# Edge-list operations on VectorE in four of eight slots instead of seven

## The chip, the cores and the metric

The kernel runs on one core of a Trainium2 chip. The core has five engines with instruction queues of their own: TensorE (PE in the profile; PEld are its weight loads), VectorE (DVE), ScalarE (ACT), GpSimd (POOL) and SyncE (SP), which issues most DMA transfers. Each queue is worked off in the order in which the kernel's program wrote it; a queue waits for another one by semaphores. The metric is the device time of one execution in microseconds. Three runs of the kernel before took 14773.6, 14776.33 and 14777.28 us; the median is 14776.33 us.

## The reference, cut to what matters

Three layers follow each other. Layer 0 is two Mamba passes (over 96 time steps, then over 32 variables) on 4 x 32 x 96 rows of 256 channels. Layer 1 has an additive attention and a graph-routed mixture of experts. Here M = 12288 rows, four batches of 3072, and 1048576 edges.

```python
# attention: every query against every key of its batch
h = tanh(q[:, :, None, :] + k[:, None, :, :] + bh)      # 3072 x 3072 x 32 per batch
a = softmax(einsum('biju,u->bij', h, Wa) + ba)
v = einsum('bij,bjd->bid', a, inputs)
# graph attention over edges (src, dst), with a loop edge for every row
e   = leaky_relu(a_src[src] + a_dst[dst], 0.2)
ee  = exp(e - segment_max(e, dst)[dst])
agg = segment_sum(h[src] * ee / segment_sum(ee, dst)[dst], dst) + b_gat
# gates: top 2 of 4 experts from layernorm(agg); then the experts
out = sum_e gate_e * (gelu(x @ W1[e] + b1[e]) @ W2[e] + b2[e])
```

The edge indices are drawn from 0 to 65535, while there are only 12288 rows. In JAX an index past the end is clamped when gathered, and dropped when used as a target of a segment sum. So most edges have the last row as source, and most have no target at all. The kernel makes lists of the edges that matter: one of edges with a real source and target, and one that only counts, per target, the edges whose source was clamped.

## The kernel before, in words

**Order.** The program writes the order of PE, ACT, DVE and POOL by hand. `Attention.units` is the clock of it. It walks over i, one **slot** each: in a slot ACT makes one tanh of a 128 x 3072 tile `th` (L1031; four queries at a time), and PE turns the tile of two slots earlier (LAG = 2) into scores (`scores`, L1004). Eight slots make a **unit** of 32 queries. The slots of a unit are numbered here by k = (i - 2) mod 8, the place of the score product that is made in the slot. `th` has three buffers, the score bank `pe` one, and the bank `pv`, which transposes and values share, one.

A unit ends so (`unit_tail`). In slot 7, after the scores, DVE takes the maximum (`nb`, L1087, "the reduce"), and ACT the exponential (`pr`, L1094). In slot 0 of the next unit PE transposes four blocks of `pr`, in slot 1 the other two, and in slot 2 it multiplies by the values (`pv`, L1110). Each of these is followed one slot later by a DVE copy out of the bank: `pT` in slots 1 and 2 (L1103), `pvs` in slot 3 (L1112). The copies are kept in `self.later` and written into DVE's queue early in the slot. Every fourth unit ends a tile of 128 queries; then `tile_tail` adds small steps in slots 3 to 7 (factors `g` and `f`, with one small exponential on ACT, L1165).

**What runs beside it.** `units` yields twice in a slot: after the tanh and after the scores. At each yield the generator `steps` in `whole` goes on. While layer 0 lasts, that is layer 0. When layer 0 has ended, the loop at L2254 takes turns:

- At the first yield of a slot it writes **list operations** of `Edges.sort` into DVE's queue. So they stand ahead of the copies of that slot, and ahead of the scores and the reduce. `sort` yields after every operation or few, with its cost in microseconds as the program's author put it down. `us_v` is the budget: it gets EDGE_US = 2.3 in each slot except slot 7 (`att.reduces`), each yielded cost is taken off, and a debt is carried on to the next slot while credit is not.
- At the second yield it writes count products of the one-hot tiles (`ed.todo`), index gathers on POOL (`columns`), and parts of the experts (`Experts.early`) by a second budget `us_t` of SLOT_US = 1.2 per slot. The experts' parts are PE products into `ph` and `po`, with a DVE bias step after them: `h` (L1933, 128 x 512) and `ko` (L1945, 128 x 512). `po` has one bank at this time, so the next product into it waits for `ko`.

**The list operations.** `sort` reads the edges in four quarters. For each quarter, 16 pieces of 256 columns are loaded by DMA into a tile `e` with two buffers and narrowed to 16 bits (L1368). Then `compact` moves the kept entries of 2048 columns to the front, eleven levels of bit, predicated copy (L1314) and up to three products or sums (L1318, L1321, L1323). A fifth compaction of 2048 columns, two of 384 and eight of 392 follow, and some index arithmetic. Up to here there are 894 yields, with costs of 480.1 us in all. Then `self.listed` is set and 232 one-hot pairs follow (L1473), each with 1.195 us of cost, limited by how fast the count products take them (`len(ed.todo) < 2`).

**Afterwards.** `units` runs out after 3072 tanhs. Then `tail` finishes the graph and the remaining experts.

Of the kernel before, what the change touches and what calls it, by code (L numbers as in the profile page):

```python
# [45 lines left out]
LAG = 2  # L46
# [14 lines left out]
G1, K1 = 8, 4  # L61
GP, GG = 12, 4
EDGE_US = 2.3
GATHER_US, HALF_US, GROUP_US, LAND_US = 1.6, 2.7, 2.0, 10.0
QUARTERS = 2, 0, 3, 1
KO_BUFS = 2
# [773 lines left out]
class Attention:  # L840
# [4 lines left out]
    def __init__(self, ctx, tc, ident, a, x1, x2, xn2T, tab_s, tab_a, keys, l0):  # L845
        self.nc = nc = tc.nc
        self.ident, self.x1, self.x2, self.xn2T = ident, x1, x2, xn2T
        self.tab_s, self.tab_e, self.tab_a = *tab_s, tab_a
        pool = lambda name, bufs, **k: ctx.enter_context(
            tc.tile_pool(name=name, bufs=bufs, side="right", **k))  # L850
        const = self.const = pool("atc", 1)
        self.rows, self.th, self.wk = pool("atr", 2), pool("atb", TH_BUFS), pool("atw", 1)
        self.ps_e = pool("ate", PE_BUFS, space=PSUM)
        self.ps_v = pool("atv", PV_BUFS, space=PSUM)

        def load(name, shape, ap):
            t = const.tile(shape, F32, tag=name, name=name)
            nc.sync.dma_start(t, ap)
            return t

        self.l0, self.kq, self.krep, self.qsel = l0, keys, keys.krep, keys.qsel
        self.wa = load("wa_blk", [P, P // (4 * R_ATT), QU], a["wa_blk"])
        self.ba = load("ba_rep", [P, 1], a["ba_rep"])
        self.wg = load("wg", [P, KC, HF], a["W_gat"].rearrange("(k p) f -> p k f", p=P))
        self.asr = load("as_rep", [P, HF], a["as_rep"])
        self.adr = load("ad_rep", [P, HF], a["ad_rep"])
        self.eps = const.tile([P, 1], F32, tag="eps1", name="eps1")
        nc.vector.memset(self.eps, 1e-5)

        self.sel = const.tile([P, QU], F32, tag="sel", name="sel")  # L870
        nc.vector.tensor_tensor(self.sel, ident[:, :QU], ident[:, QU:2 * QU], ALU.add)
        for q in range(2, P // QU):
            nc.vector.tensor_tensor(self.sel, self.sel, ident[:, q * QU:(q + 1) * QU], ALU.add)
        self.state = [{} for _ in range(B)]

        self.extra, self.entry, self.col, self.asked, self.normed = 0.0, 0, 0, 0, 0
        self.now, self.reduces = None, False
        self.mark = const.tile([P, 1], F32, tag="mark", name="mark")

        self.later = []  # L880
# [111 lines left out]
    def units(self, side):  # L992


        nc = self.nc
        todo, behind = [], []
        NK = QU // R_ATT
        PER = TOK // R_ATT

        def scores(pe, k, th):  # L1000
            for j in range(2):
                for q in range(NQT):
                    c0 = q * KQ + j * KQ // 2
                    nc.tensor.matmul(pe[q * QU:(q + 1) * QU, j, :KQ // 2], self.wa[:, k, :],  # L1004
                                     th[:, c0:c0 + KQ // 2], start=(k == 0), stop=(k == NK - 1))

        def beside():
            while side:
                try:
                    return next(side[0])  # L1010
                except StopIteration:
                    side.pop(0)

        i = 0
        while i < B * PER + LAG or todo or self.later:
            b, col = self.entry, self.col = divmod(i, PER)
            if self.waits(b, col):

                yield
                late, self.later = self.later, []
                for f in late:
                    f()
                yield
                beside()
                continue
            if b < B:
                s = self.state[b]
                th = self.th.tile([P, TOK], F32, tag="th", name="th")  # L1030
                nc.scalar.activation(th, s["krep"], AF.Tanh, bias=s["qsel"][:, col:col + 1])  # L1031
                behind.append(th)
                self.now = th
            self.reduces = behind and (i - LAG) % NK == NK - 1
            yield
            late, self.later = self.later, []
            for f in late:
                f()
            busy = tail = None
            if behind and i >= LAG:  # L1040
                n, k = divmod(i - LAG, NK)
                if k == 0:
                    pe = self.ps_e.tile([P, 2, JB], F32, tag="pe", name="pe")
                scores(pe, k, behind.pop(0))
                if k == NK - 1:
                    tail = self.unit_tail(*divmod(n, TOK // QU), pe)
                    busy = True

            self.extra = 0.0 if tail or not todo else getattr(todo[0], "us", 0.0)
            yield  # L1050
            if tail:

                for f in todo:
                    f()
                todo = tail()
            elif todo and hasattr(todo[0], "us"):
                if not todo[0].full:
                    beside()
                todo.pop(0)()
                busy = True  # L1060
            elif todo:
                todo.pop(0)()

            if b < B and col == LAG + 3:
                self.load_values(b)
            if b < B and LAG + 4 <= col < LAG + 10:
                self.normalize_values(b, col - LAG - 4)
            if b and col == LAG + 10:
                side.append(self.after(b - 1, *AFTER[-1]))
            side += [self.after(b, t0, t1) for t0, t1 in AFTER[:-1]  # L1070
                     if b < B and col == t1 * P // R_ATT + LAG + 10]
            if busy is None:
                beside()
            i += 1
        side.append(self.after(B - 1, *AFTER[-1]))
# [156 lines left out]
class Edges:  # L1232
# [97 lines left out]
    def sort(self):  # L1330
# [4 lines left out]
        with ExitStack() as ctx:  # L1335
# [157 lines left out]
            while self.todo:  # L1493
                yield EDGE_US
            v.tensor_copy(self.cnt, pc)
# [339 lines left out]
class Experts:  # L1835
# [62 lines left out]
    def output(self, h, q0, w2):  # L1898
        po = self.bank(self.ps_o, [P, 2, C], "po")
        for q in range(2):  # L1900
# [3 lines left out]
            yield po  # L1904

    def early(self, units, a, place):


# [299 lines left out]
def whole(tc, a, dram, out):  # L2208
# [12 lines left out]
    with ExitStack() as ctx:  # L2221
        actx, lctx, ectx = ExitStack(), ExitStack(), ExitStack()
        with tc.manual_schedule(engines={E.PE, E.Activation, E.DVE, E.Pool}):
# [5 lines left out]
            att, side = None, []  # L2229
            late = {}  # L2230

            def steps():
                nonlocal att

                for done in l0.run():
                    if done is not None:
                        b, i = done
                        if att is None and i == max(PARTS):
                            att = Attention(actx, tc, ident, a, x1, x2, xn2T, (tab_s, tab_e), tab_a,
                                            keys, l0)  # L2240
# [8 lines left out]
                ed = late["ed"] = Edges(ctx, ectx, tc, a, tab_e, tab_a)  # L2249
# [2 lines left out]

                us_v = us_t = 0.0
                while True:  # L2254
                    us_v = min(us_v, 0.0) + (0.0 if att.reduces else EDGE_US)
                    while lists and us_v > 0 and len(ed.todo) < 2 and "krep" in att.state[B - 1]:
                        us = next(lists, None)
                        if us is None:
                            lists, late["listed"] = None, True
                        else:  # L2260
                            us_v -= us
                    yield
                    if columns is None and ed.listed and att.normed >= B - 1:
                        columns, turn = ed.columns(), 1
                    if columns:
                        att.pace()
                        turn = 3 - turn
                        for f, k, c in columns[:turn]:
                            f(k, c)
                        del columns[:turn]  # L2270
                    us_t = min(us_t, SLOT_US) + SLOT_US - att.extra
                    if ed.todo and us_t > 0:
                        ed.todo.pop(0)()
                        us_t -= G1 * PRODUCT_US
                    if units is None and att.entry == B - 1 == att.normed:

                        units = late["units"] = ex.early(
                            [(i, e) for i in range(NBLK_X - NBLK_X // B) for e in range(NEXP)
                             if (i, e) not in ex.done], a, att.krep[B % 2])
                    while units and us_t > 0:  # L2280
                        us_t -= next(units, 1.0) or 0.0
                    yield

            flow = steps()
            while not side:
                next(flow)
# [96 lines left out]
```

## Time and profile before

| what | value |
|---|---|
| median of three runs | 14776.33 us |
| the profiled execution's own time | 14803.64 us |
| span, first to last instruction | 14801.9 us |
| mean granted TensorE clock | 0.897 |
| list operations in DVE's queue (first load to first one-hot) | 11303 to 12168 us |
| one-hots | 12168 to 13355 us |
| last reduce of the attention | 13857 us |

The profiled execution took 27.3 us longer than the median of the runs. "Busy" is the time in which an engine worked; "idle before" is the time an engine stood still ahead of a group of instructions, with the name of what ended most of it. A wait is put down to the semaphore that came last. DVE, ACT and POOL start their instructions in the queue's order, so an instruction that waits holds up all behind it.

### The profile page before, as it was taken

The page shows a single profiled execution, that of the slowest core. Times are in us where ns is not written, and L with a number is a line of the kernel's source. Part 1 is how long each engine was busy: PE and PEld are TensorE (multiplying, and loading weights), DVE is VectorE, ACT ScalarE, POOL GpSimd, SP SyncE. Part 2 cuts the span into 40 slices and gives each one's busy share as a digit, 9 for nine tenths or more (in the row PEclk, how much of TensorE's full clock was granted, in tenths as well). Part 3 has the DMA queues.
Part 4 walks back from the last instruction along what each step waited for, and adds up shares of the span by engine and source line. Part 5 has one row for each costly group of instructions (what it writes and reads, how often), then busy time and mean ns, then how long its engine had stood idle before and what let it go on. Part 6 is the DMA issues. An engine that isn't in the chain of part 4 may idle for free.

```text
span 14801.9 us, 224787 instructions
## 1 busy us (share of the span) xinstructions
PE 11378.9 (77%) x86704; PEld 5164.8 (35%) x86704; DVE 10505.3 (71%) x15265; ACT 12306.2 (83%) x9676; POOL 9078.2 (61%) x7108
## 2 busy tenths in 40 slices
PE   5777767777777777778887777788876778988888
PEld 2333332222222333333333233333332334443466
DVE  7888887777777777777778777667786783331376
ACT  3445559999999899999998899999998889999522
POOL 5777767777777667777676677657762005550272
PEclk8888988888888888899998888999988999999999
DMA  6777765445455444455554444445542000010233
GB/s 208 228 228 229 230 198 148 148 149 151 149 152 154 147 146 149 152 153 153 151 153 147 151 148 149 131 127 150 155 148 89 27 19 13 9 22 18 60 105 117
DMA packets 1206752, 1984.20 MB, mean 134 GB/s; under 512 B 419364, under 2 KB 655396, under 8 KB 1200548
## 3 DMA queue, kind: packets, MB, share of 16 engines
q1 hardware_dynamic: 1174948, 1963.77, 43.4%
q0 software_dynamic: 30720, 5.96, 0.8%
q8 instruction: 682, 11.17, 0.3%
q14 instruction: 402, 3.29, 0.1%
HBM read 1859.14 MB, written 110.18 MB: 133 GB/s over the span
## 4 chain that ended last, share of the span: by engine, by line


## 5 line engine op out<-in xcount | busy, mean ns | idle before, releaser
L1031 ACT ACTIVATE th<-krep,qsel 128x3072 f32<-128x3072 f32 x3072 | 8676.3, 2849 | 373.6 <-PE pe L1004 346.7
L1004 PE MATMUL pe<-th,wa_blk 128*32 128x384 f32 x49152 | 5026.5, 536 | 1633.0 <-ACT pr L1094 1528.5
L514 POOL TENSOR_TENSOR h<-h,bC 128x768 f32<-128x768 f32 x2048 | 3766.0, 1840 | 2718.9 <-DVE h L507 2267.0
L507 DVE TENSOR_TENSOR_SCAN h<-dA,dB 128x384 f32<-128x384 f32 x3008 | 2707.2, 941 | 862.6 <-ACT dA L469 629.1
L1004 PEld LDWEIGHTS pe<-th,wa_blk 128*32 128x32 f32 x49152 | 1471.5, 116 | 4140.5 <-issue 1932.0
L482 DVE TENSOR_TENSOR dB<-bB,dtu 128x768 f32<-128x768 f32 x1912 | 1812.4, 948 | 207.1 <-ACT dtu L557 134.5
L521 POOL TENSOR_TENSOR h<-h 128x768 f32<-128x768 f32 x752 | 1414.4, 1881 | 53.6
L533 PE MATMUL py<-h,ident 128*128 128x384 f32 x2176 | 946.9, 567 | 485.9 <-POOL h L514 485.1
L469 ACT ACTIVATE dA<-dt,t_A 128x380 f32<-128x380 f32 x2048 | 1118.4, 569 | 216.1 <-DVE h L507 131.2
L469 ACT ACTIVATE dA<-dt,d_A 128x372 f32<-128x372 f32 x2048 | 1103.7, 562 | 133.0 <-DVE h L502 61.4
L1110 PE MATMUL pv<-xn,pT 128*32 128x257 f32 x18432 | 1104.1, 387 | 127.3 <-DVE pT L1103 126.9
L502 DVE TENSOR_TENSOR_SCAN h<-dA,dB 128x768 f32<-128x768 f32 x544 | 947.7, 1751 | 144.8 <-ACT dA L469 93.8
L1169 POOL TENSOR_SCALAR sf<-sel,f 128x32 f32<-128x32 f32 x384 | 151.1, 417 | 1296.9 <-ACT f L1165 1296.4
L1103 DVE COPY pT<-ptw 128x512 f32<-128x512 f32 (+1 forms) x768 | 420.5, 548 | 683.6 <-PE ptw L1101 672.8
L1110 PEld LDWEIGHTS pv<-xn,pT 128*32 128x32 f32 x18432 | 582.2, 112 | 708.7 <-DVE pT L1103 255.1
L522 POOL TENSOR_TENSOR h<-h 128x384 f32<-128x384 f32 x752 | 783.8, 1042 | 59.0
L523 POOL TENSOR_TENSOR y<-y,h 128x384 f32<-128x384 f32 x752 | 777.2, 1033 | 59.0
L533 PEld LDWEIGHTS py<-h,ident 128*128 128x128 f32 x2176 | 424.6, 212 | 952.2 <-POOL h L514 726.6
L1087 DVE TENSOR_REDUCE nb<-pe 128x1 f32<-128x768 f32 x384 | 363.2, 946 | 446.5 <-PE pe L1004 428.6
L1253 POOL DMA_INDIRECT gd<-tab_a,di x480 | 491.3, 1024 | 165.3 <-issue 162.3
L1101 PE MATMUL ptw<-ident,pr 128*128 128x128 f32 x2304 | 473.6, 323 | 100.4 <-DVE pT L1103 45.7
L1112 DVE COPY pvs<-pv 128x257 f32<-128x257 f32 x384 | 159.8, 416 | 516.4 <-PE pv L1110 462.5
(326 smaller groups left out, 15255.2 us busy)
## 6 DMA issues: line engine op xcount, KB each, us to landing
bB<-bc SPq DMA_DIRECT2D x2048, 384.0 KB
bC<-bc SPq DMA_DIRECT2D x2048, 384.0 KB
x<-x SPq DMA_DIRECT2D x321, 128.0 KB
all<-kept SPq DMA_DIRECT2D x40, 1024.0 KB
kept<-ko SPq DMA_DIRECT2D x43, 512.0 KB
xt<-xn2T SPq DMA_DIRECT2D x41, 512.0 KB
qsel<-xn2T SPq DMA_DIRECT2D x75, 256.0 KB
kept<-eo SPq DMA_DIRECT2D x150, 128.0 KB
```

Source lines behind the costliest of these rows:

```text
L469: nc.scalar.activation(inner(dA[:, s * T:(s + 1) * T] if alone else self.dA[s][:, :T]), inner(blk["dt"][:, e, :]), AF.Exp, scale=blk["w"][ ...
L482: nc.vector.tensor_tensor(dB, blk["bB"].pop(j), z["dtu"].unsqueeze(1).to_broadcast([P, SB, T]), ALU.mult)
L502: nc.vector.tensor_tensor_scan(flat(h), dA[:, :SB * T], flat(dB), 0.0, ALU.mult, ALU.add)
L507: nc.vector.tensor_tensor_scan(h[:, s, :], self.dA[s][:, :T], dB[:, s, :], 0.0, ALU.mult, ALU.add)
L514: nc.gpsimd.tensor_tensor(h, h, blk["bC"].pop(j), ALU.mult)
L521: nc.gpsimd.tensor_tensor(h0, h0, h1, ALU.add)
L522: nc.gpsimd.tensor_tensor(h0[:, 0, :], h0[:, 0, :], h0[:, 1, :], ALU.add)
L523: nc.gpsimd.tensor_tensor(y[e], y[e], h0[:, 0, :], ALU.add)
L533: nc.tensor.matmul(z["py"], self.ident, h[:, s, :], start=(i == 0), stop=(i == DS - 1))
L1004: nc.tensor.matmul(pe[q * QU:(q + 1) * QU, j, :KQ // 2], self.wa[:, k, :], th[:, c0:c0 + KQ // 2], start=(k == 0), stop=(k == NK - 1))
L1031: nc.scalar.activation(th, s["krep"], AF.Tanh, bias=s["qsel"][:, col:col + 1])
L1110: nc.tensor.matmul(pv[q * QU:(q + 1) * QU, :C + 1], pT[:, i, q * QU:(q + 1) * QU], s["xn"][:, q * NK + i, :], start=(i == 0), stop=(i == N ...
```

## The change

A constant EDGE_MORE = 0.1 is added to the cost of each list operation. While the lists are made (`not ed.listed`), the budget is no longer 2.3 us in each of slots 0 to 6, but 4.6 us in slots 0, 4, 5 and 6 (LIST_STEPS), and nothing in slots 1, 2, 3 and 7. `att.step_of` carries the slot's number. Once the one-hots begin, the budget per slot is the old one again; the 0.1 us stays. What the operations are, and their order among themselves, does not change; only how many of them stand in which slot.

```diff
 EDGE_US = 2.3
+EDGE_MORE = 0.1
+LIST_STEPS = 0, 4, 5, 6
...
-        self.now, self.reduces = None, False
+        self.now, self.reduces, self.step_of = None, False, 0
...
             self.reduces = behind and (i - LAG) % NK == NK - 1
+            self.step_of = (i - LAG) % NK
             yield
...
                 while True:
-                    us_v = min(us_v, 0.0) + (0.0 if att.reduces else EDGE_US)
+                    us_v = min(us_v, 0.0) + (
+                        (0.0 if att.reduces else EDGE_US) if ed.listed else
+                        (2 * EDGE_US if att.step_of in LIST_STEPS else 0.0))
                     while lists and us_v > 0 and len(ed.todo) < 2 and "krep" in att.state[B - 1]:
                         us = next(lists, None)
                         if us is None:
                             lists, late["listed"] = None, True
                         else:
-                            us_v -= us
+                            us_v -= us + EDGE_MORE
                     yield
```

## The prediction

> **What bounds the kernel now.** I read the page first, then busy time by stage, then the waits of ACT, the groups and the order of time of single units. The profile's chain of waits is empty in this run, so the path is argued from the waits.
>
> ```profile
> span 14801.9 us, 224787 instructions
> ...
> DVE  7888887777777777777778777667786783331376
> ACT  3445559999999899999998899999998889999522
> ```
>
> From the sixth slice on ACT is busy nine tenths or more, with dips; the last two thirds of the span go at the pace of its tanhs. One dip is in slices 31 to 33, where the list operations stand (11303 to 12168 us). By stage (PE, PEld, DVE, ACT, POOL):
>
> ```profile
> 11477.00:11933.00 456.00, 361.81 (x3414) 151.91 (x3412) 356.02 (x404) 408.50 (x169) 10.28 (x16) 0.94 0.09 28
> 11933.00:12168.00 235.00, 171.25 (x1474) 66.89 (x1478) 213.46 (x674) 181.03 (x76) 4.52 (x8) 0.89 0.05 15
> 12168.00:13355.00 1187.00, 1055.11 (x11066) 505.69 (x11062) 432.32 (x840) 1129.24 (x461) 686.09 (x1008) 0.95 0.10 15
> ```
>
> ACT stands still for 47.5 us in the stage of long list operations, 54.0 us in that of short ones (there DVE is busy for 91%), and only 5% of the time under the one-hots. What ends its waits from 11303 to 12168 us:
>
> ```profile
> ACT th L1031 <- PE pe L1004: 91.8, 53, 11.7
> ACT pr L1094 <- DVE nb L1087: 41.6, 8, 16.4
> ACT f L1165 <- DVE f L1162: 15.3, 4, 6.6
> ```
>
> So 150 us of ACT time are open here, and that is all that the change can win: 1.0% of the run. Most is PE being late (its scores stand behind products that wait for copies in DVE's queue), a quarter the reduce being late itself. The groups in the same stretch:
>
> ```profile
> L1031 ACT ACTIVATE th<-krep,qsel 128x3072 f32<-128x3072 f32 x239 | 667.9, 2850 | 92.3 <-PE pe L1004 91.8
> ...
> L1902 PE MATMUL po<-krep,h 128*128 128x256 f32 x256 | 69.8, 419 | 37.9 <-DVE ko L1945 36.1 <-DVE count L1290 1.8
> ```
> ```profile
> L1087 DVE TENSOR_REDUCE nb<-pe 128x1 f32<-128x768 f32 x30 | 28.6, 954 | 41.0 <-PE pe L1004 41.0
> ...
> L1368 DVE TENSOR_SCALAR pair<-e 128x256 uint16<-128x256 int32 x64 | 19.5, 313 | 53.2 <-DMA e<-in_edges 52.6
> ...
> L1314 DVE COPY_PREDICATED pair<-bit,pair 128x2047 f32<-128x2047 uint16 x5 | 13.0, 2595 | 0.1
> ...
> L1318 DVE TENSOR_TENSOR go<-move,bit 128x2047 uint16<-128x2047 uint16 x5 | 6.1, 1224 | 0.0
> ```
>
> A unit needs 8 tanhs of 2.850 and an exponential of 0.89, 23.7 us of ACT. PE was 36.1 us behind `ko`. Each edge load costs DVE 53.2/64 = 0.83 us of waiting besides its 0.31. Now a unit that begins with a late reduce, in DVE's order of time:
>
> ```profile
> 11593.11 0.96 DVE L1087 TENSOR_REDUCE nb<-pe 128x1 f32<-128x768 f32 x1 [5.25 <-PE pe L1004]
> ...
> 11599.05 0.67 DVE L1103 COPY pT<-ptw 128x512 f32<-128x512 f32 x1
> ...
> 11601.74 0.42 DVE L1103 COPY pT<-ptw 128x256 f32<-128x256 f32 x1
> ...
> 11605.09 0.43 DVE L1112 COPY pvs<-pv 128x257 f32<-128x257 f32 x1 [0.44 <-PE pv L1110]
> ```
>
> From the reduce's end (11594.07) to the start of `pvs` it takes 11.0 us, with some 10 us of list operations between; but PE's chain of scores, transposes, scores and values fills nearly all of that time. The other late reduce (11324.15, `pvs` at 11336.86) gives 11.8. Under no list operations the shortest I see is 10.3 (reduce 13530.08, `pvs` 13541.37).
>
> **The change part by part.** It adds and removes no instruction; PE, ACT, POOL and SP keep their order. DVE's list operations move, and with them the edge loads that SP issues: their two buffers make each load wait for the DVE operation two before it, so the loads follow wherever DVE stands. SP's later transfers (expert inputs, kept blocks) are queued behind them as now.
>
> *How much per unit.* Before, 7 x 2.3 = 16.1 us of written cost; 480.1/16.1 = 29.8 units. After, 4 x 4.6 = 18.4, and (480.1 + 894 x 0.1)/18.4 = 31.0 units. The one more unit is a unit of the same tanhs and costs only its waits. A level of a long compaction is written as 0.68 + 2.27 + 3 x 1.14 = 6.4 and takes 0.69 + 2.60 + 3 x 1.23 = 7.0 us; so a unit held 17.6 us of DVE time and holds 18.4/6.9 x 7.0 = 18.7 now. The eight short compactions are written as 85.4 us (432 yields) and took 147.2 from one operation's start to the next. They filled 5.3 units with 27.8 us each; now (85.4 + 43.2)/18.4 = 7.0 units with 21.0 each. That is the gain in it.
>
> *Where in the unit.* Slot 0's share (4.9 us) ends where the shares of slots 0 and 1 ended before, so the first `pT` is no earlier. The second `pT` and `pvs` lose the 2.3 us ahead of each. But three quarters now lie between `pvs` and the reduce: walking the costs through the budget gives 13.8 us per unit in the long stage and 15.8 in the short, where 7.0 to 13.1 lay before. DVE can't begin them earlier, since `pvs` stands ahead of them. So a unit from reduce to reduce is: 11.2 to `pvs` (near the two late rows) + 0.43 + 13.8 + 0.95 (an `h` or `ko`, and a quarter of the tile's steps, from what stood there before) + 0.95 for the reduce = 27.3 us. ACT needs 23.7; it stands still for 3.6 us. In the short stage, 5.6. Behind the reduce wait the exponential, all later tanhs, and PE's next scores.
>
> *Long stage, 11477 to 11933 us.* 14 units without edge loads; in two of them the experts' gelu (two of 1.9 us with two table loads of 1.28) gives ACT other work. 12 x 3.6 = 43. Two units have 16 edge loads: one with 4 in slot 0 and 12 in slot 4 (18.4 us late), one with all in slots 5 and 6 (14.4). Sum 76, against 47.5 now: +29.
>
> *Short stage.* Nine units, one with gelu: 8 x 5.6 = 45 against 54: -9.
>
> *Beginning, 11303 to 11477 us* (layer 0 is ending): 16 loads fall into slots 5 and 6 as now (15.5); the two following units are 4 us late each, the next quarter's loads are split over two units, 8 + 12; with the 6.6 at `f` that makes 50 against 49.4 now: +1.
>
> *PE behind its own copies.* `ko` stands in DVE's queue behind the list operations of its slot, and the next `po` product waits for it on PE, ahead of the next scores. In slots 4 and 5 this ends before the reduce could anyway. In slot 6 it comes on top: in the late unit above PE had 3.70 us of `po` and 1.50 of scores left after `ko`, 5.2 us. Of 16 `ko` I take two there: +10. Bounds: none, and all 16 (+83).
>
> *Costed at nothing.* The 0.1 us on one-hots: the written cost would allow 16.1/1.295 = 12 pairs a unit; they go at about 5 (1187 us for 232), held by the count products. That lists end a unit later: one-hots and gathers end some 500 us before the last reduce (13355 against 13857). If that cover were gone, a unit would cost 24 us. Expert units done early: their budget counts slots, and the number of slots is the same.
>
> Sum: +29 - 9 + 1 + 10 = +31 us on the profiled 14803.6 (27.3 above the median of the runs), so 14776.3 + 31 = 14807.
>
> The largest unknown is the time to `pvs`. One us changes 12 long and 8 short units: 20 us. Bounds 10.3 (-18) and 13 (+36; expert products between lead to that in many units now). I take 11.2 because both late rows are near.
>
> [...] ACT waits for DVE and PE while DVE is busy for 78% (356 of 456 us). [...]
>
> **The rivals.**
>
> 1. *The copies let PE run ahead* (faster). For it: 91.8 us of ACT's waits are PE's, and nothing stands ahead of the second `pT` and `pvs` any more. If `pvs` came at 8.5 us, the sum would be 31 - 20 x 2.7 = -23, and without the `ko` term -33: 14743. It decides at 9.7 us (31/20 = 1.55 below 11.2). Against it: no unit in the trace goes below 10.3.
> 2. *PE behind `ko` often* (slower). As many as 8 of 16 in slot 6: 31 - 10 + 42 = +63: 14839; all of them 14880. For it: the 36.1 us of today, with half the list work per slot.
> 3. *Nothing to measure.* The DVE time is only moved and waits change names: today's 150 us stay, 14776. For it: the total of the list work is the same, and the two stages have opposite signs.
>
> **How the numbers follow.** A difference under 0.2%, 30 us, is about what a measurement of this kernel can't tell from none. The forecast (late reduce, +31, own range 14785 to 14845) gets 0.56; it ends slower by over 30 us half of the time (0.29), otherwise within. Rival 1 gets 0.16: 0.11 faster and 0.05 within. Rival 2 gets 0.18, all slower. Rival 3 gets 0.10, within. So faster 0.11, same 0.42, slower 0.47. The range leaves out half of rival 1 and the end of rival 2: 14760 to 14875.
>
> **What would show it.** Right: ACT's wait for `nb` grows from 41.6 us to over 100, its wait for PE falls from 91.8 to under 50; units of 27 us in the long stage, and of 30 instead of 32 in the short; lists end one unit later. Wrong: `pvs` earlier than 10 us after the reduce, or ACT's waits for PE not falling. The forecast fails if DVE finds more cover in slots 0 to 3 than I see, or if expert products meet the list runs at another phase.

## Result and profile after

The changed kernel takes 14875.44 us (median of four runs, 14873.35 to 14881.23); the kernel before took 14776.81 us in the runs beside it. The ratio is 1.0069, with a 95% interval of 1.0057 to 1.0081: 98.6 us slower. The forecast was slower by 31 us (14807). So the direction was right, the size a third of what came, and the time lies 0.4 us above the upper end of the range (14875).

The page after, of the profiled execution (14873.7 us):

```profile
span 14871.9 us, 224787 instructions
...
DVE  6888887777777777777778777677776673332376
ACT  3445559999999899999998899999997779999622
```

The dip in ACT's row has become deeper and stands in slices 31 to 33 as before. The list operations now last from 11301 to 12290 us, 990 us instead of 863. By stage (PE, PEld, DVE, ACT, POOL, granted clock, DMA):

```profile
11301.00:11484.00 183.00, 99.39 (x944) 36.34 (x940) 123.62 (x168) 123.22 (x51) 3.16 (x5) 0.76 0.17 52
```
```profile
11484.00:11974.00 490.00, 348.29 (x3010) 142.78 (x3010) 330.15 (x372) 368.03 (x151) 19.92 (x16) 0.84 0.08 24
```
```profile
11974.00:12290.00 316.00, 238.03 (x2135) 98.30 (x2135) 243.11 (x708) 250.62 (x102) 3.95 (x8) 0.88 0.06 16
```

Before, the first of the three stages, which the prediction only names by its sum, read:

```profile
11303.00:11477.00 174.00, 103.66 (x973) 37.10 (x962) 120.01 (x167) 124.64 (x52) 2.73 (x5) 0.77 0.18 55
```

Stretch less ACT's busy time is ACT's stand. It was 49, 48 and 54 us in these three stages, 151 in all; it is 60, 122 and 65 now, 247 in all. The difference, 96 us, is the 98.6 us of the result to within the spread of the runs. (The two profiled executions themselves lie only 70 us apart, because that of the kernel before was 27 us above its runs.) What ends ACT's waits, from 11301 to 12290 us:

```profile
ACT pr L1097 <- DVE nb L1090: 122.9, 23, 20.7
ACT th L1033 <- PE pe L1006: 80.7, 61, 8.0
ACT f L1168 <- DVE f L1165: 29.2, 7, 6.5
ACT h L1941 <- DVE h L1936: 12.7, 2, 12.3
```

The exponential's wait for the reduce has tripled (41.6 before). The wait for PE has hardly fallen (91.8), the wait for the small factor `f` has doubled, and one is new: the experts' gelu waits for its own bias step `h` in DVE's queue. What PE waits for, apart from the exponential:

```profile
PE po L1905 <- DVE ko L1948: 63.4, 10, 19.7
PE ph L1897 <- DVE h L1936: 29.2, 10, 7.3
PE pf L1163 <- DVE g L1157: 21.8, 7, 3.8
PE ptw L1104 <- DVE x L1184: 19.0, 6, 6.5
...
PE ptw L1104 <- DVE pT L1106: 4.8, 3, 3.8
```

Before, the same list read:

```profile
PE po L1902 <- DVE ko L1945: 36.1, 10, 15.5
PE pv L1110 <- DVE pT L1103: 36.1, 18, 8.3
PE ptw L1101 <- DVE pT L1103: 19.0, 12, 3.8
...
PE pf L1160 <- DVE g L1154: 6.9, 4, 2.5
```

This is the change in two lists. PE's waits for `pT` went from 55.1 to 4.8 us: that is what the empty slots 1 to 3 give. In their place PE waits for whatever else stands in DVE's queue in slots 4 to 6: `ko`, `h`, `g`. A single unit of the long stage, DVE in order of time:

```profile
11872.82 0.95 DVE L1090 TENSOR_REDUCE nb<-pe 128x1 f32<-128x768 f32 x1
...
11879.15 0.69 DVE L1106 COPY pT<-ptw 128x512 f32<-128x512 f32 x1 [2.52 <-PE ptw L1104]
11880.95 0.42 DVE L1106 COPY pT<-ptw 128x256 f32<-128x256 f32 x1 [1.11 <-PE ptw L1104]
11885.02 0.43 DVE L1115 COPY pvs<-pv 128x257 f32<-128x257 f32 x1 [3.64 <-PE pv L1113]
11885.36 0.68 DVE L1288 TENSOR_SCALAR bit<-keep 128x2048 uint16<-128x2048 uint16 x1
...
11902.68 0.75 DVE L1936 TENSOR_SCALAR h<-ph,b1e 128x512 f32<-128x512 f32 x1
11903.33 0.96 DVE L1090 TENSOR_REDUCE nb<-pe 128x1 f32<-128x768 f32 x1
```

and ACT in the same unit:

```profile
11877.67 19.80 ACT L1033 ACTIVATE th<-krep,qsel 128x3072 f32<-128x3072 f32 x7 [0.22 <-PE pe L1006]
11904.32 0.90 ACT L1097 ACTIVATE pr<-pe,nb 128x768 f32<-128x768 f32 x1 [6.85 <-DVE nb L1090]
```

DVE stands still for 7.3 us ahead of the three copies, where list operations stood before. Then it works without a gap from 11885.0 to 11904.3: list operations with two `h` among them, and at their end the reduce. ACT has made all eight tanhs by 11897.5 and waits 6.85 us.

### The profile page after: what moved, and what is told of

It reads as the page before. It is cut to its first block, busy times and chain, and to the rows that moved or that the text cites. A ratio compares the mean times of both kernels' runs of the same rounds, so it can differ in the third digit from the quotient of the medians.

```text
span 14871.9 us, 224787 instructions
## 1 busy us (share of the span) xinstructions
PE 11379.6 (77%) x86704; PEld 5167.4 (35%) x86704; DVE 10503.6 (71%) x15265; ACT 12323.6 (83%) x9676; POOL 9086.6 (61%) x7108
## 4 chain that ended last, share of the span: by engine, by line
ACT 39%; PE 27%; DVE 17%; issue 8%; POOL 5%; DMA 3%; SPq 1%; DVEq 0%; POOLq 0%; ACTq 0%
ACT th L1033 26%; PE pe L1006 11%; ACT dA L471 6%; PE pv L1113 3%; DVE h L509 3%; DVE h L504 3%; DVE dB L484 2%; POOL h L516 2%; PE po L1905 2%; ACT pr L1097 2%; PE pz L578 2%; PE py L535 1%; PE ph L1897 1%; PE ptw L1104 1%; PE pa L1653 1%
## 5 line engine op out<-in xcount | busy, mean ns | idle before, releaser
L1113 PE MATMUL pv<-xn,pT 128*32 128x257 f32 x18432 | 1087.6, 384 | 99.0 <-DVE pT L1106 98.6
```

The lines of the kernel that those rows point to most:

```text
L1113: nc.tensor.matmul(pv[q * QU:(q + 1) * QU, :C + 1], pT[:, i, q * QU:(q + 1) * QU], s["xn"][:, q * NK + i, :], start=(i == 0), stop=(i == N ...
```

## Experiments

ACT's stand in the list stretch (first edge load to first one-hot) is the main reading of all of them.

| kernel | list cost per unit, slots | stand, us | ratio to before (95%) |
|---|---|---|---|
| before | 16.1, slots 0 to 6 | 151 | 1 |
| changed | 18.4, slots 0, 4, 5, 6; EDGE_MORE | 247 | 1.0069 (1.0057 to 1.0081) |
| EDGE_MORE only | 16.1, slots 0 to 6 | 105, 106 | 1.0006; 0.9973 |
| four slots only | 18.4, slots 0, 4, 5, 6 | 313 | 1.0119 (1.0102 to 1.0136) |
| spread | 18.4, slots 0 to 6; EDGE_MORE | 124, 123 | 1.0028; 0.9984 |
| smaller run | 13.8, slots 0, 4, 5, 6; EDGE_MORE | 194 | 1.0039 (1.0024 to 1.0053) |
| three load buffers | 16.1, slots 0 to 6 | 133 | 0.9987 (0.9978 to 0.9997) |
| EDGE_MORE, three buffers | 16.1, slots 0 to 6 | 92, 84 | 0.9965; 0.9961 |

**The level.** The kernel before was profiled once more. (A sample is here a set of kernels timed in turn on one chip, with the kernel before among them.)

> The kernel before, unchanged, profiled once more, because the first profiled execution of it took 14803.6 us where the median of its runs is 14776.3. If profiling or that execution costs 27 us, this one lands near 14800 again; if the first was an odd execution, it lands near 14777, and then the list stretch (865 us from first load to first one-hot) and the wait of the exponential for the reduce (41.6 us) should come out within 5 us of the first, and the 27 us be in another stage.

It took 14803.1 us, and its 15 other runs of that sample 14795.16 to 14819.75, median 14807.4. In later samples it took 14767 to 14770. So the level of a sample moves by 40 us. Whether the 27.3 us that the prediction noted between profile and runs are of that kind is not shown. The list stretch was the same to 1 us (stand 151). The changed kernel was timed in a second sample too.

> The changed kernel, unchanged, timed in turn with the kernel before on one more chip, since the kernel before took 14776 us in its first runs and 14807 in later ones. If the change's cost is what the list stretch shows (ACT still for 247 us instead of 151), the ratio is again about 1.007 whatever the level. If the one-hot stretch, where the profiles of single executions differ by 70 us with the same instructions, is what decides, the ratio moves by as much as 0.004 and the profile shows a one-hot stretch of some 1255 us instead of 1183.

14872.82 against 14770.43: 1.0069 again (1.0052 to 1.0086). Its stand in the list stretch was 248 us.

**One half of the change at a time.** First EDGE_MORE alone, in the old slots.

```diff
-                            us_v -= us
+                            us_v -= us + EDGE_MORE
```

> Only EDGE_MORE (0.1 us on each list operation); the slots stay 0 to 6 with 2.3 us each. 569.5/16.1 = 35.4 units instead of 29.8, so less list work per unit: 16.3 us in the long stage, 147/(128.6/16.1) = 18.4 in the short one (27.8 before). Theory that the run of list operations between the sums copy and the reduce makes ACT wait: that run is 7 to 8 us in both stages now, and the reduce is on time; ACT's waits in the list stretch fall from 150 to some 110 us, time 14735 (-40). Rival that EDGE_MORE is what made the changed kernel slow (more units under list work, each with waits of 4 to 5 us): 5.6 more units at 4 us, 14800 (+25).

The list stretch did what the first theory said: 105 us of stand instead of 151. Yet the time was that of the kernel before (1.0006, 0.9996 to 1.0015), because ACT stood still under the one-hots for 119 us where it had been 58. There this version differs only by 0.1 us on each one-hot pair, which the changed kernel has too (1183 us for that stretch), so it was run again.

> EDGE_MORE alone once more, beside another sample of the kernel before. In its first profile ACT stood still for 45 us less than before in the list stretch, and 61 us more under the one-hots, where nothing of the schedule is different but the slot in which they begin. If the one-hot part belongs to the kernel, the stretch is again near 1257 us (ACT still for 119 us) and the time that of the kernel before. If it was that execution, the stretch is near 1180 us and the time 40 us below the kernel before (ratio 0.997).

The stand in the list stretch was the same (106), the one-hot stretch 1188 us with 51 us of stand, and the ratio 0.9973 (0.9962 to 0.9983): 35 us faster. ACT's waits in the list stretch:

```profile
ACT th L1032 <- PE pe L1005: 67.0, 56, 8.5
ACT pr L1095 <- DVE nb L1088: 24.8, 6, 9.3
ACT f L1166 <- DVE f L1163: 10.7, 2, 6.1
```

All three are below those of the kernel before. The rival, that EDGE_MORE does the harm, is out. Now the four slots alone:

```diff
-EDGE_MORE = 0.1
+EDGE_MORE = 0.0
```

> Only the four slots with 4.6 us, EDGE_MORE set to 0. 480.1/18.4 = 26.1 units, the runs between sums copy and reduce are about 15 us in the long stage and 24 in the short one (31.7 us of list time per unit there). Theory of the late reduce: short-stage units of 37 us and more, waits for the reduce over 130 us in all; time 14895 (+120), slower than the changed kernel's 14875. Rival that EDGE_MORE is the harmful part: 14780.

1.0119, 171 us slower; it took 14978.52 where 14895 was expected. The waits:

```profile
ACT pr L1097 <- DVE nb L1090: 184.0, 23, 20.9
ACT th L1033 <- PE pe L1006: 91.8, 59, 8.5
ACT f L1168 <- DVE f L1165: 34.6, 6, 10.0
```

The slots do the harm, more than all of it (162 us of stand above the kernel before, where the changed kernel has 96); EDGE_MORE takes part of it back.

**Place or volume.** The four slots also carry more work in a unit (18.4 instead of 16.1). The same volume spread evenly:

```diff
-                        (2 * EDGE_US if att.step_of in LIST_STEPS else 0.0))
+                        (0.0 if att.reduces else 8 * EDGE_US / 7))
```

> The changed kernel's volume (18.4 us of written cost per unit, EDGE_MORE 0.1), but spread evenly: 2.63 us in each of slots 0 to 6 while the lists are made. As many units (31) as in the changed kernel, only the place differs. Theory of place: the run from sums copy to reduce is 8 us instead of 14 to 16, the wait for the reduce falls from 123 us to under 45, and the time is that of the kernel before or a little better: 14765 (14740 to 14785). Rival of volume (21 us of list work per unit is too much for VectorE wherever it stands): 14860 to 14880, with waits that only move from the reduce to the copies.

> The spread version once more, for the same question: under the one-hots its instructions stand in the same slots as in the changed kernel, and ACT stood still there for 123 us in the first profile and 46 to 51 in the two of the changed kernel. If it was that execution, the one-hot stretch is near 1180 us now, and the ratio to the kernel before 0.997 to 1.000 instead of 1.0028; if it belongs to the kernel, 1.0028 again.

In both profiles the list stretch had 123 to 124 us of stand, half of the changed kernel's 247, with the same number of units. The time fell apart in the same way as with EDGE_MORE alone: 1.0028 (1.0015 to 1.0040) in the sample in which the one-hot stretch had 123 us of stand, 0.9984 (0.9974 to 0.9993) in the other, with 48. In the second sample the time is 14744.2 us, within the range that the theory of place gave; in the first it was 14840.3, where the kernel before took 14807.4. Waits of the list stretch in the second:

```profile
ACT th L1033 <- PE pe L1006: 75.5, 55, 6.0
ACT pr L1097 <- DVE nb L1090: 34.1, 6, 16.3
```

The wait for the reduce is 34 us instead of 123. Volume is not free, but cheap: with EDGE_MORE and seven slots, 16.1 us a unit gave 105 us of stand and 18.4 gave 123. The same 18.4 us moved into four slots gives 247.

**A smaller run in the same four slots.**

```diff
-                        (2 * EDGE_US if att.step_of in LIST_STEPS else 0.0))
+                        (1.5 * EDGE_US if att.step_of in LIST_STEPS else 0.0))
```

> The changed kernel with 1.5 times the old budget instead of twice (3.45 us in slots 0, 4, 5 and 6, EDGE_MORE 0.1): the same four slots, a smaller run. 569.5/13.8 = 41.3 units. The run between the sums copy and the reduce is 10.3 us in the long stage and 11.9 in the short one, instead of 13.8 and 15.8. Theory that the length of this run against the room that is left makes the wait: with the sums copy at 12.4 us, 12.4 + 0.43 + 10.3 + 1.9 = 25.0, 1.3 us late instead of 4.8; the wait of the exponential for the reduce falls from 123 us to about 50 (bursts of edge loads left), ACT's stand in the list stretch from 247 to 150 us or less, time that of the kernel before within 30 us. Rival that the four slots as such are bad (PE's and ACT's waits stay with any run in slots 4 to 6): a fall in proportion to the run only, stand of 200 us or more, time +60.

Here the theory missed. The stand was 194 us and the ratio 1.0039: about halfway, in proportion to the run, and near the rival's numbers.

```profile
ACT pr L1097 <- DVE nb L1090: 89.6, 20, 15.5
ACT th L1033 <- PE pe L1006: 78.7, 66, 7.4
```

There is no sharp point below which a run is free. In the list stretches the time from `pvs` to the reduce was 14.2 us in the mean of the units without loads and gelu (16.6 in the changed kernel), and the `pvs` copy began 9 to 18 us after the reduce; so part of the units are late with any run. Over the spread version, the smaller run, the changed kernel and the four slots alone, that mean was 10.5, 14.2, 16.6 and 20.2 us, and the stand 123, 194, 247 and 313 us: some 20 us of stand for each microsecond, though the list stretches differ too (25 to 40 units). No run tells the part of slot 0 from that of slots 4 to 6.

**The experts' share.** Their early parts were held back while lists are made, in both kernels, with more budget afterwards. Each was profiled in one execution, and ACT's stand is all that is read from it.

```diff
-                    us_t = min(us_t, SLOT_US) + SLOT_US - att.extra
+                    us_t = min(us_t, SLOT_US) + SLOT_US - att.extra + (0.25 if ed.listed else 0.0)
...
-                    while units and us_t > 0:
+                    while units and us_t > 0 and ed.listed:
```

> The kernel before, with the experts' early parts held back while the lists are made (and 0.25 us more budget per slot for them once the one-hots begin, to catch up). What counts is the list stretch. If the products into po and ph, with their DVE steps ko and h behind list operations, are what makes PE late, ACT stands still there for about 115 us instead of 151; if it is only the copies and the reduce, for 145 or more.

> The changed kernel with the same hold on the experts. By the prediction's own sum without experts a unit of the long stage is 11.0 to the sums copy + 0.43 + 13.8 + 0.2 + 0.95 = 26.4 us, 2.7 late, and one of the short stage 4.7 late; ACT then stands still for about 160 us in the list stretch instead of 247, with units that begin their sums copy at 10.5 to 11.5 us. The rival: the experts' parts do not matter, the sums copy still comes at 13 us, and ACT stands still for 230 us or more.

The stands were 129.5 and 196 us. Both lie between the numbers of theory and rival. The difference between the kernels shrinks from 96 to 67 us: some 30 us of the change's cost come by way of the experts' products and DVE steps, and the other 67 remain without them. The sums copy came at 11.8 us after the reduce in the mean, a little later than expected, and the units took 27.4 us in the long stage and 29.0 in the short one, where 26.4 and 28.4 were expected. The waits of the changed kernel without experts:

```profile
ACT pr L1097 <- DVE nb L1090: 126.5, 28, 16.4
ACT th L1033 <- PE pe L1006: 37.5, 47, 7.1
```

The reduce's wait stays in full; the wait for PE halves. To see whether the products ahead of `pvs` or behind it matter, they were barred from slots 0 to 2 alone:

```diff
-                    while units and us_t > 0:
+                    while units and us_t > 0 and (ed.listed or att.step_of > 2):
```

> The changed kernel with the experts' early parts barred from slots 0, 1 and 2 of a unit while the lists are made (they go on in slots 3 to 7). If their products ahead of the sums copy are the missing time, the copy comes at 11.7 us as in the run without experts, instead of 12.5, a unit takes 29 us instead of 30, and ACT stands still for about 220 us in the list stretch instead of 247: ratio 1.005. If they only move behind the copy and lengthen the way from there to the reduce, the unit stays at 30 us, the stand at 240 us or more: ratio 1.007.

`pvs` at 11.8 us instead of 12.5, units of 29.5 us instead of 30.1, a stand of 228, ratio 1.0055 (1.0039 to 1.0070). So products ahead of `pvs` explain 19 of the 96 us; the first theory holds, a little short of its numbers.

**The edge loads.** Three buffers instead of two:

```diff
-                with tc.tile_pool(name="ee", bufs=2) as pool:
+                with tc.tile_pool(name="ee", bufs=3) as pool:
```

> The kernel before with three buffers instead of two for the edge loads, nothing else. DVE waits 0.83 us per load now (53 us in all, in bursts of 16 loads). If a load's latency bounds them, three buffers bring the wait down to 0.4 us or less per load and DVE's wait to 20 to 30 us; ACT's waits of 15.5 and 16.4 us for the reduce behind such bursts fall to about 9 each, time 20 us lower (ratio 0.9985). If the wait is the transfers' rate, nothing changes.

```profile
L1368 DVE TENSOR_SCALAR pair<-e 128x256 uint16<-128x256 int32 x64 | 18.9, 312 | 31.0 <-DMA e<-in_edges 30.5
```

DVE's wait fell from 52.6 to 30.5 us (0.82 to 0.48 us a load), the stand from 151 to 133, the time to 0.9987 of the kernel before. So the time of a single load bounds the bursts and not the rate of the transfers, as expected.

**A version that beats both.** EDGE_MORE and three buffers, seven slots.

> A version that should beat both: seven slots of 2.3 us as before, EDGE_MORE 0.1, and three buffers for the edge loads. The two gains are in different units (three buffers took 17 us off ACT's stand in the stage of long operations, EDGE_MORE 28 us off that of the short ones and 18 of the long ones): ACT still for about 85 to 90 us in the list stretch instead of 151, time 55 us below the kernel before (ratio 0.996). If the one-hot stretch grows by 60 us as in the first run of EDGE_MORE alone, the time is that of the kernel before.

> EDGE_MORE and three buffers, seven slots, once more: ratio 0.996 to 0.997 to the kernel before. If the execution of 36215 us came from this kernel (more edges lost than the lists hold, and so the general path taken), it comes again in some of its executions; if from outside, all lie within 40 us of each other.

0.9965 (0.9951 to 0.9978) and 0.9961 (0.9947 to 0.9975): 14719.7 and 14710.8 us, 48 and 59 us below the kernel before; beside the changed kernel's 1.0069 the ratio is lower by 0.0104 and 0.0108. One execution of the first sample took 36215 us and is not in these numbers; none of the second did. What that was stays open.

## Why the prediction was right or wrong

- **Which side, and by what.** Right. The long run between `pvs` and the reduce makes the reduce late; ACT's wait for it went to 122.9 us, where "over 100" was named as the sign. The four slots alone, the spread version and EDGE_MORE alone separate the parts as the steps had them: harm by place, gain by the 0.1 us.
- **The gain in the short stage** by fewer operations per unit is real: EDGE_MORE alone takes ACT's stand there (from the first short compaction on) from 43 to 15 us. In the changed kernel the place gives it back. The step had -9 us for the short stage; it was 65 against 54, +11.
- **The step that failed: the sum for a unit, 27.3 us, and in it "11.2 to `pvs`".** By the sum a unit takes 27.3 us in the long stage and 29.3 in the short one. Measured over the units of these two stages without loads and gelu, nine of each, it was 30.1 us in both. In the long stage `pvs` began 12.9 us after the reduce (11.2 in the sum), and from there to the next reduce it took 16.2 us (15.2 in the sum); in the short stage it was 12.1 (11.2) and 17.1 (17.2). Of the two rows behind the 11.2, the one with 11.0 had 2.0 us of the experts' products ahead of `pvs`, the one with 11.8 none; the 18 units had 2.3 us in the mean. With these products barred from slots 0 to 2 (0.5 us left) `pvs` began at 11.8 us instead of 12.5 in the mean of both stages. So some 0.7 of the missing 1.3 us are theirs; the rest stays open.
- **What the misses add up to.** ACT stood still for 60, 122 and 65 us in the three stages, where the steps had 50, 76 and 45: 76 us more. Counted from one reduce's end to the next, the units without loads and gelu make 39 of them (19 units with 127 us, where the step had 12 x 3.6 + 8 x 5.6 = 88). Three units of the long stage with a gelu, which the step had at nothing, make 18, the beginning 10, the two units with edge loads 5. Ten of the 76 had been set down for `ko` apart, so the sum missed 66 us (151 + 31 = 182; 247 measured).
- **The half clock.** After a late reduce PE has been idle, and its first 16 scores take up to 2.79 us instead of 1.50 (2.2 in the mean of the 18 units, 1.8 in such units before). Of the two rows behind the 11.2, the one with 11.0 had its first scores in 1.50 us, the one with 11.8 in 2.79; I took a figure near the first. The granted clock of the long stage fell to 0.84 (0.94 before).

```profile
11756.85 2.79 PE L1006 MATMUL pe<-th,wa_blk 128*32 128x384 f32 x16 [22.24 <-ACT pr L1097]
...
11764.65 1.50 PE L1006 MATMUL pe<-th,wa_blk 128*32 128x384 f32 x16
```

The same two stretches with PE's busy time, its granted clock and the DMA's share:

```profile
11756.85:11759.64 2.79, 2.79 (x17) 0.50 0.00 0
11764.65:11766.15 1.50, 1.50 (x21) 1.00 0.00 0
```

The first, after 22.24 us of waiting, ran at half the clock of the second (0.50 against 1.00). That the lower clock makes `pvs` later is not shown: among the 18 units, those with their first scores in 1.5 us began `pvs` after 12.3 us in the mean, those with 2.5 us or more after 12.5.

- **A wait that was not on the list.** The gelu waits for the last `h`, which stands behind a quarter's 16 edge loads and the list operations of slots 4 to 6: 12.7 us, 12.3 of them in one unit. I had counted the gelu as cover for ACT, and here it was none. But it cost little of its own, for the reduce of that unit was no earlier:

```profile
11751.03 0.95 DVE L1090 TENSOR_REDUCE nb<-pe 128x1 f32<-128x768 f32 x1
11751.90 0.74 DVE L1936 TENSOR_SCALAR h<-ph,b1e 128x512 f32<-128x512 f32 x1
```
```profile
11752.68 1.91 ACT L1941 ACTIVATE h<-h 128x2048 f32<-128x2048 f32 x1 [12.34 <-DVE h L1936]
```

The reduce ended at 11751.98, so without the gelu ACT would have had to wait about as long for it.

- **PE behind its own copies.** The mechanism was named and taken at +10 for `ko` alone. Waits for `ko`, `h` and `g` rose from 44 to 114 us together. Not all of it reaches ACT: with the experts held back in both kernels, the difference falls by some 30 us. So the second rival was part of the truth beside the forecast, not instead of it. One of the three units with a gelu shows it: `ko` stands behind the whole run, PE's products and scores come after it, and then the reduce, for which ACT waited 9.98 us.

```profile
11967.80 0.69 DVE L1948 TENSOR_TENSOR ko<-po,krep 128x512 f32<-128x512 f32 x1
11974.29 0.96 DVE L1090 TENSOR_REDUCE nb<-pe 128x1 f32<-128x768 f32 x1 [5.80 <-PE pe L1006]
```
```profile
11968.54 3.78 PE L1905 MATMUL po<-krep,h 128*128 128x256 f32 x8 [8.57 <-DVE ko L1948]
11972.25 1.96 PE L1006 MATMUL pe<-th,wa_blk 128*32 128x384 f32 x16
```
```profile
11975.28 0.90 ACT L1097 ACTIVATE pr<-pe,nb 128x768 f32<-128x768 f32 x1 [9.98 <-DVE nb L1090]
```

- **"Its wait for PE falls from 91.8 to under 50".** Wrong: 80.7. The waits for `pT` did vanish, as the first rival said, and others took their place.
- **The first rival** (PE runs ahead) needed `pvs` at 9.7 us. It came at 12.5 in the mean; that rival is out.
- **The bounds.** They were 10.3 and 13 for `pvs`, each priced alone. The upper end of the range took in `pvs` at 13 or the copies, but not both, and nothing for the units with a gelu.
- **DVE at 78%, with ACT waiting for it.** Only the groups of list operations were made smaller or larger, no instruction was: the same volume in seven groups a unit cost 124 us of ACT's stand, in four 247.
- **Costed at nothing.** Right: the one-hots end at 13473 us, 469 us before the last reduce, and the 0.1 us there changes nothing (1183 us against 1187).
- **A reading.** ACT's row stands at nine tenths from the seventh slice on, not from the sixth; nothing rests on it.

## What to carry to other kernels

When work is moved out of the way of one dependency on an in-order queue, add up what then stands between the last thing the queue must wait for and the next thing others wait for; that run against the room is the price, and every other consumer on the queue (here a gelu's bias, 12.7 us of ACT's waits, and a product's eviction `ko`, 63.4 us of PE's) joins the waiters. Take the length of such a chain from the mean over many units, with its slowest kinds in it, rather than from one or two clean rows. Spreading and honest costs for small operations gave what bunching was meant to give: EDGE_MORE in the old slots, with a third load buffer, is 0.4% faster than before.

## What the hardware showed that I had not expected

With the same instructions in the same order, the one-hot stretch took 1256 us in one profiled execution of the spread version and 1179 in another (ACT's stand 123 and 48 us); EDGE_MORE alone did the same, 1257 and 1188. Both long ones were of the sample in which the kernel before took 14807 us, but the profile of the kernel before in that sample had a short stretch. In the long executions the granted clock of the stretch was 0.93 instead of 0.94, and with EDGE_MORE alone ACT's tanhs waited 79 us for PE's scores instead of 47. What decides it stays open.
